# A shifted-window attention and depthwise-convolution kernel: how the first image is brought in, and where one normalization per image stands

## The chip, the cores and the metric

The kernel runs on one core of a Trainium2 chip. The metric is the device time of one execution in microseconds; the executions of a kernel are summed up by their median. A core has TensorE (PE, with weight loads PEld), VectorE (DVE), ScalarE (ACT), GpSimd (POOL) and SyncE (SP). Each engine runs its own instructions in the order in which the program has them. SP, ACT and POOL also issue DMA transfers.

## The reference

The input `x` has shape 16 x 56 x 56 x 384 in float32. Two layers follow each other, each with a residual:

```
x = x + attention(group_norm(x))     # 32 groups of 12 channels, statistics per image
x = x + depthwise(group_norm(x))     # 3x3, kernel clipped to [-1, 1] and made binary

attention(x):
    x = roll(x, (-3, -3))
    q, k, v = x @ w_qkv.T            # 12 heads of 32
    per 7x7 window: softmax(q k^T / sqrt(32) + rel_pos_table[POS] + mask) v
    out = roll(out @ w_out.T + b_out, (3, 3))
```

The statistics of the first norm need a whole image, so nothing of an image's attention starts before all of it has been read.

## The kernel before

An image is cut into eight strips (`NS`) of seven rows; strip `s` of the program is strip `s % 8` of image `s // 8`. Channels lie on the partitions, in three blocks (`NC`) of 128. A strip has eight windows, worked on in two halves, so the main loop runs over 256 half strips `u`.

`fetch(s)` reads a strip from memory into one of two landing tiles `xls` by transfers on SP's queue: six for most strips, twelve for the last strip of an image, because the shift wraps it around the image. `load(s, c)` turns it to channel-major on TensorE (`pl`), copies it to `xs` on ScalarE, and takes statistics on VectorE.

The norm of an image has two parts. `norm_gather` combines the statistics on VectorE and moves them through DRAM (`mvd`, then `gt`), so that the twelve channels of a group lie on one partition. `norm_scale` does the arithmetic of a group on GpSimd, and moves scale and shift back through DRAM (`cod`, then `coef`).

The start, in program order: clear the unused part of the landing tiles and fetch strips 0 and 1; clear the padded tiles (`clear_more`); load the relative position table row by row (`load_bias`: 49 transfers of one row, one that doubles the rows, and two for the mask, all on GpSimd's queue); load strips 0 to 7, each followed by the fetch two strips on, with the weights' twelve transfers after the last fetch; gather and norm of image 0 on SP's queue; transposes of the weights (`load_weights`: per block three TensorE transposes and one copy, eight of the twelve copies on VectorE, four on ScalarE); the depthwise taps (`load_depthwise`: one transfer for the taps and three for the output bias on ScalarE's queue, six VectorE operations, a transpose, a copy); the bias additions; then `normalize(0)` on ScalarE and the first query and key matmuls.

In the main loop, `heavy(u)` gives a list of slots of work for TensorE, and `run` issues them one by one. After the first three slots stands a transpose of the attention weights each (`pp`); after slot three stands `attend`, which multiplies by the values (`po`) and copies the output `ot` on ScalarE. Before slot 0 stands `scores(u + 1)`; before the third transpose stands `softmax(u + 1)`. "Light" work, from a plan with due times, goes behind the slot in which it falls due: a due time `w` goes out when `w - u` is at most `(i + 1) / slots`. The plan holds the fetches and loads of the next image (`plan_load`) and the convolution of the image before (`plan_conv`).

In the second half of a strip the first three slots hold the value matmuls of the next strip. Three more hold the projection of the strip before, unless the strip is the first of an image. `normalize(s + 2)`, three ScalarE operations that write `xn`, stands in the fifth slot (index `NC + 1`). Where the strip is the first of an image, the list has two empty slots in place of the projection, and the normalization comes in the last of five slots, after `attend`. This happens once per image, at `u = 16 b + 1`.

Of the kernel before, what the change touches and what calls it, by code (L numbers as in the profile page):

```python
# [9 lines left out]
F32 = mybir.dt.float32  # L10
AF = mybir.ActivationFunctionType
ALU = mybir.AluOpType
AX = mybir.AxisListType

WIN = 7
SHIFT = WIN // 2
GROUPS = 32
# [16 lines left out]
def kernel(  # L34
# [12 lines left out]
    nc = tc.nc  # L47
# [60 lines left out]

    hps = [const.tile([P, BR + 2, W + 2], F32, tag=f"hp{n}", name=f"hp{n}") for n in range(2)]

    def clear():
        for xl in xls:
            nc.gpsimd.memset(xl[:, NL - 1, :], 0.0)

    def clear_more():
        nc.gpsimd.memset(power, -0.5)
        for t in (xn, qk[:, :, ST:], vt, *es, *hps):
            nc.gpsimd.memset(t, 0.0)

    staged = []  # L120

    def fetch_weights():

        rows = [w[r * P : (r + 1) * P, :] for w in (w_qkv, w_out) for r in range(w.shape[0] // P)]
        for n in range(0, len(rows), NC):
            wl = xpool.tile([P, NC, ST], F32, tag="x", name=f"wl_{n}")
            for k in range(NC):
                nc.sync.dma_start(wl[:, k, :C], rows[n + k])
            staged.append(wl)
# [27 lines left out]

    loaded_bias = []

    def load_bias():  # L160

        rel = ypool.tile([P, NC, WIN, R], F32, tag="y", name="rel").rearrange("q c h w -> q (c h w)")[:, : T * NH]
        nc.gpsimd.memset(rel, 0.0)
        flat = rel.rearrange("q (a n) -> q a n", a=WIN)
        for q in range(T):
            qr, qc = divmod(q, WIN)
            first = (WIN - 1 - qr) * REL + (WIN - 1 - qc)
            row = rel_table[first : first + 1, :]
            src = bass.AP(
                tensor=row.tensor,  # L170
                offset=row.offset,
                ap=[[NH, 1], [REL * NH, WIN], [1, WIN * NH]],
            )
            nc.gpsimd.dma_start(flat[q : q + 1], src)
        nc.gpsimd.dma_start(flat[HT : HT + T], flat[0:T])
        mask = ypool.tile([P, NC, WIN, R], F32, tag="y", name="mask").rearrange("q c h w -> q (c h w)")[:, : 2 * T]
        mask = mask.rearrange("q (v k) -> q v k", v=2)
        nc.gpsimd.memset(mask, 0.0)
        for w in range(2):
            nc.gpsimd.dma_start(mask[w * HT : w * HT + T], wmask[0:T, :, 0:T])  # L180
        loaded_bias[:] = [rel, mask]

    def add_bias():
        rel, mask = loaded_bias
# [14 lines left out]
    def norm_gather(key, queue):  # L199

        st = stats.pop(key)
        name = "%d_%d" % key
        mv = small.tile([P, NC, 2], F32, tag="mv", name=f"mv{name}")
        for c in range(NC):
            nc.vector.bn_aggr(mv[:, c, :], st[:, c].rearrange("p s k -> p (s k)"))
        if key[0]:
            nc.vector.tensor_tensor(mv[:, :, 0], mv[:, :, 0], bo_sb, ALU.add)
        by_channel = dram.tile([C, 2], F32, tag="mvd", name=f"mvd{name}")
        queue.dma_start(by_channel.rearrange("(c p) k -> p c k", p=P), mv)
        gt = small.tile([GROUPS, GS, 2], F32, tag="gt", name=f"gt{name}")  # L210
        queue.dma_start(gt.rearrange("g n k -> g (n k)"), by_channel.rearrange("(g n) k -> g (n k)", n=GS))
        parts[key] = gt

    def norm_scale(key, queue):

        gt = parts.pop(key)
        name = "%d_%d" % key
        g = small.tile([GROUPS, 4], F32, tag="g", name=f"g{name}")
        mean, var, rstd, shift = (g[:, n : n + 1] for n in range(4))
        dev = small.tile([GROUPS, GS], F32, tag="dev", name=f"dev{name}")  # L220
        pool = nc.gpsimd

        def fold(x):

            n = GS
            while n > 1:
                half = n // 2
                pool.tensor_tensor(x[:, :half], x[:, :half], x[:, n - half : n], ALU.add)
                n -= half

        pool.tensor_copy(dev, gt[:, :, 0])
        fold(dev)
        pool.tensor_scalar(mean, dev[:, 0:1], 1.0 / GS, None, ALU.mult)
        pool.tensor_tensor(dev, gt[:, :, 0], mean.to_broadcast([GROUPS, GS]), ALU.subtract)
        pool.tensor_tensor(dev, dev, dev, ALU.mult)
        pool.tensor_tensor(dev, dev, gt[:, :, 1], ALU.add)
        fold(dev)
        pool.tensor_scalar(var, dev[:, 0:1], 1.0 / GS, EPS, ALU.mult, ALU.add)
        pool.tensor_tensor(rstd, var, power[:GROUPS], ALU.pow)
        pool.tensor_tensor(shift, mean, rstd, ALU.mult)  # L240
        pool.tensor_scalar(shift, shift, -1.0, None, ALU.mult)
        both = small.tile([GROUPS, GS, 2], F32, tag="both", name=f"both{name}")
        pool.tensor_copy(both, g[:, 2:4].unsqueeze(1).to_broadcast([GROUPS, GS, 2]))
        by_channel = dram.tile([C, 2], F32, tag="cod", name=f"cod{name}")
        queue.dma_start(by_channel.rearrange("(g n) k -> g (n k)", n=GS), both.rearrange("g n k -> g (n k)"))
        coef = small.tile([P, NC, 2], F32, tag="coef", name=f"coef{name}", bufs=4)
        queue.dma_start(coef, by_channel.rearrange("(c p) k -> p c k", p=P))
        coefs[key] = coef
# [3 lines left out]

    xs = {}

    def fetch(s):
        b, r = divmod(s, NS)
        xl = xls[s % 2]
        first = r * WIN + SHIFT
        for odd in range(2):
            t, end = 0, (WIN + 1 - odd) // 2  # L260
            while t < end:
                row = (first + odd + 2 * t) % H
                n = min(end - t, (H - row + 1) // 2)
                rows = x[b, row : row + 2 * n - 1 : 2].rearrange("t w c -> w t c")
                here = xl[odd * W : (odd + 1) * W, t : t + n, :]
                for lo, hi in ((SHIFT, SHIFT + 48), (SHIFT + 48, W), (W, R)):
                    nc.sync.dma_start(here[lo - SHIFT : hi - SHIFT], rows[lo % W : (hi - 1) % W + 1])
                t += n

    def load(s, c):  # L270
        b, r = divmod(s, NS)
        if (0, b) not in stats:
            stats[0, b] = small.tile([P, NC, NS, 6], F32, tag="st0", name=f"st0_{b}", bufs=1)
        if c == 0:
            xs[s] = xpool.tile([P, NC, ST], F32, tag="x", name=f"x_{s}")
        pt = bank(f"pl_{s}_{c}")
        for t in range(NL):

            n = min(LT, max(ST - t * LT, HT + 1))
            nc.tensor.transpose(  # L280
                pt[:, t * LT : t * LT + n], xls[s % 2][:n, t, c * P : (c + 1) * P], ident[:n, :n]
            )
        nc.scalar.copy(  # L283
            xs[s][:, c, :].rearrange("p (w r c) -> p r w c", r=WIN, c=WIN),
            pt[:, :ST].rearrange("p (r w c) -> p r w c", w=NW, c=WIN),
        )
        nc.vector.bn_stats(stats[0, b][:, c, r, :], xs[s][:, c, :])  # L287
# [286 lines left out]
    def heavy(u):  # L574

        s, half = divmod(u, UPS)
        if half == 0:
            todo = [[] for _ in range(2 * NC)]
            if s + 1 < B * NS:
                for m in range(2 * NC):  # L580
                    todo[m].append((query_key, (s + 1, m)))
            for n, m in enumerate((0, 1, 4, 5)):
                todo[m].append((by_key, (s, n)))
            if s > 0 and s % NS == 0:
                todo += [[(project, (s - 1, m))] for m in range(NC)]
        else:
            todo = [[] for _ in range(NC)]
            if s + 1 < B * NS:
                for m in range(NC):
                    todo[m].append((value, (s + 1, m)))  # L590
            if s > 0 and s % NS:
                todo += [[(project, (s - 1, m))] for m in range(NC)]
            else:
                todo += [[], []]
            if s + 2 < B * NS:
                todo[NC + 1].append((normalize, (s + 2,)))
        return todo

    def run(todo):
# [3 lines left out]

    with tc.manual_schedule():
        clear()
        fetch(0)
        fetch(1)
        clear_more()
        load_bias()
        for s in range(NS):  # L610
            for c in range(NC):
                load(s, c)
            if s + 2 < NS:
                fetch(s + 2)
            if s + 2 == NS - 1:
                fetch_weights()
        norm_gather((0, 0), nc.sync)
        norm_scale((0, 0), nc.sync)
        for n in range(NC + 1):
            load_weights(n)  # L620
        load_depthwise()
# [78 lines left out]
```

## Time and profile before

| What | Value |
|---|---|
| Median of four executions | 4734.1 us (4730.68 to 4735.7) |
| The profiled execution | 4730.68 us, span 4728.9 us |
| Busy share of the span | PE 96%, PEld 63%, DVE 84%, ACT 52%, POOL 11% |
| Mean granted TensorE clock | 0.979 |
| First transfer of a strip issued | 1.33 us |
| Statistics ready, `mvd` issued | 41.85 us |
| Group arithmetic on GpSimd | 50.29 to 56.75 us |
| First query matmul (`pq`) | 60.85 us |

In the lines of the profile, times are microseconds from the start of the span. A group names its line in the code, the engine, the operation, the output and the inputs, and how often it occurs; the bracket at the end holds the idle time of the engine before it and what ended that. "Issue" is time in which an engine waited for nothing that the profile shows. A busy TensorE is not one at full speed, since matmuls are pipelined.

### The profile page before, as it was taken

To read this page: it belongs to the slowest core of one execution; us is meant where nothing else is said; L and a number is where in the kernel's file an instruction comes from. 1 tells how busy PE (TensorE), PEld (TensorE's weight loads), DVE (VectorE), ACT (ScalarE), POOL (GpSimd) and SP (SyncE) were. 2 spreads that over 40 slices of the span, in tenths; PEclk is the share of its full clock that TensorE was granted. 3 is DMA by queue.
4 is the path that set the end of the run, shared out by engine and by line. 5 is a ranking of instruction groups with operands and counts; after the bars stand their busy time and mean duration, and the time that the engine had idled before them with its cause. 6 is when DMAs were issued, how large, how long until landed. Compare 5 with 4: busy or idle time off the path is not lost.

```text
span 4728.9 us, 146228 instructions
## 1 busy us (share of the span) xinstructions
PE 4527.0 (96%) x65895; PEld 2997.2 (63%) x65895; DVE 3951.6 (84%) x4367; ACT 2473.4 (52%) x4805; POOL 527.5 (11%) x1214
## 2 busy tenths in 40 slices
PE   6999999999999999999999999999999999999981
PEld 4666666666666666666666666666666666666651
DVE  4557888888888888888888888888888888888898
ACT  3445555555555555555555555555555555555543
POOL 3001110111101011110111101011110111101000
PEclk9999999999999999999999999999999999999995
DMA  3112222222222323223232222223223232222223
GB/s 75 48 28 60 79 63 84 68 70 83 68 66 79 80 63 84 66 71 88 60 78 83 63 70 79 79 64 84 65 72 88 60 78 83 68 65 67 63 68 95
DMA packets 168067, 337.71 MB, mean 71 GB/s; under 512 B 24290, under 2 KB 126187, under 8 KB 167442
## 3 DMA queue, kind: packets, MB, share of 16 engines
q1 hardware_dynamic: 142528, 246.48, 20.2%
q0 software_dynamic: 24464, 81.86, 4.9%
q8 instruction: 517, 8.47, 0.8%
q14 instruction: 108, 0.88, 0.1%
q10 hardware_dynamic: 450, 0.02, 0.0%
HBM read 169.69 MB, written 158.47 MB: 69 GB/s over the span
## 4 chain that ended last, share of the span: by engine, by line
PE 93%; DVE 3%; ACT 2%; issue 1%; DMA 1%; POOL 0%; SPq 0%; ACTq 0%; DVEq 0%; POOLq 0%
PE pq L307 34%; PE pv L320 17%; PE py L429 16%; PE ps L351 6%; PE pp L386 6%; PE po L407 5%; PE pk L333 4%; PE pl L280 3%; PE px L528 3%; DVE o L517 2%; DMA xl<-in_x_dram 0%; ACT e L375 0%; ACT hp L492 0%; ACT pt L392 0%; DMA mvd<-mv 0%
## 5 line engine op out<-in xcount | busy, mean ns | idle before, releaser
L307 PE MATMUL pq<-xn,wq_t 128*128 128x392 f32 x4608 | 1700.5, 504 | 26.6 <-ACT xn L296 17.6
L517 DVE SCALAR_TENSOR_TENSOR o<-hp,dw_t,o 128x784 f32<-128x784 f32 x1536 | 1572.6, 1026 | 29.9 <-ACT o L504 10.7
L307 PEld LDWEIGHTS pq<-xn,wq_t 128*128 128x128 f32 x4608 | 816.2, 190 | 488.3 <-ACT xn L296 24.8
L314 ACT COPY qk<-pq 128x392 f32<-128x392 f32 x768 | 373.7, 487 | 1149.7 <-PE pq L307 1147.9
L320 PE MATMUL pv<-xn,wq_t 128*128 128x392 f32 x2304 | 840.3, 499 | 0.0
L429 PE MATMUL py<-ot,wo_t 128*128 128x392 f32 x2304 | 814.5, 499 | 0.3 <-ACT xo L529 0.3
L377 DVE TENSOR_REDUCE total<-e 128x24 f32<-128x1176 f32 x256 | 352.6, 1377 | 371.6 <-ACT e L375 370.8
L429 PEld LDWEIGHTS py<-ot,wo_t 128*128 128x128 f32 x2304 | 417.4, 190 | 258.8 <-ACT ot L416 2.4
L320 PEld LDWEIGHTS pv<-xn,wq_t 128*128 128x128 f32 x2304 | 404.0, 188 | 224.7
L327 ACT COPY vt<-pv 128x392 f32<-128x392 f32 x384 | 190.0, 495 | 623.9 <-PE pv L320 623.9
L386 PEld LDWEIGHTS pp<-ident,e 113*128 113x128 f32 x3072 | 356.6, 140 | 174.4 <-issue 100.0
L359 DVE SCALAR_TENSOR_TENSOR t<-ps,bias 128x1176 f32<-128x1176 f32 x256 | 352.6, 1378 | 111.2 <-PE ps L351 111.2
L386 PE MATMUL pp<-ident,e 113*128 113x113 f32 x3072 | 423.0, 259 | 4.9 <-DVE e L380 3.5
L449 POOL COPY y<-y 128x63 f32<-128x63 f32 x128 | 32.4, 253 | 3143.9 <-DVE y L437 3143.9
L392 ACT COPY pt<-pp 128x392 f32<-128x392 f32 x768 | 370.0, 482 | 5.8 <-PE pp L386 5.2
L380 DVE TENSOR_TENSOR e<-e,inv 128x1176 f32<-128x1176 f32 x256 | 354.6, 1385 | 8.8
L370 DVE TENSOR_TENSOR t<-t,top 128x1176 f32<-128x1176 f32 x256 | 354.1, 1383 | 8.8
L369 DVE TENSOR_REDUCE top<-t 128x24 f32<-128x1176 f32 x256 | 352.8, 1378 | 8.8
L407 PEld LDWEIGHTS po<-pt,v 49*32 49x32 f32 x24576 | 246.2, 105 | 157.9 <-ACT pt L392 81.3
L351 PEld LDWEIGHTS ps<-qk 32*64 32x64 f32 x24576 | 281.7, 131 | 93.7 <-issue 59.6
L351 PE MATMUL ps<-qk 32*64 32x49 f32 x24576 | 315.1, 228 | 14.2 <-issue 14.1
L287 DVE BATCH_NORM_STATS2 st<-x 128x6 f32<-128x392 f32 x384 | 216.2, 563 | 124.2 <-ACT x L283 119.5
(79 smaller groups left out, 4347.7 us busy)
## 6 DMA issues: line engine op xcount, KB each, us to landing
mid<-y POOLq DMA_DIRECT2D x112, 619.5 KB, 4.0
out_dram<-xo SPq DMA_DIRECT2D x192, 336.0 KB
xb<-mid SPq DMA_DIRECT2D x96, 472.0 KB
xb<-mid SPq DMA_DIRECT2D x96, 442.5 KB
xl<-in_x_dram SPq DMA_DIRECT2D x112, 288.0 KB
xl<-in_x_dram SPq DMA_DIRECT2D x112, 216.0 KB
out_dram<-xo SPq DMA_DIRECT2D x64, 168.0 KB
xl<-in_x_dram SPq DMA_DIRECT2D x48, 144.0 KB
```

The source lines that it names most:

```text
L307: nc.tensor.matmul(pq[:, :ST].rearrange("p (w t) -> p w t", t=T), wq_t[:, c, m * P : (m + 1) * P], xn[:, c, :, :T], start=(c == 0), stop=( ...
L314: nc.scalar.copy(qk[:, m, :ST], pq[:, :ST])
L320: nc.tensor.matmul(pv[:, :ST].rearrange("p (w t) -> p w t", t=T), wq_t[:, c, 2 * C + m * P : 2 * C + (m + 1) * P], xn[:, c, :, :T], start= ...
L351: nc.tensor.matmul(pp[r * HT : (r + 1) * HT, i, k0 : k0 + T], qk[part, j, q0 : q0 + HT], qk[part, NC + j, q0 : q0 + T], start=True, stop=True,
L369: nc.vector.tensor_reduce(top, tr, AX.X, ALU.max)
L370: nc.vector.tensor_tensor(tr, tr, top.unsqueeze(2).to_broadcast([P, 2 * NH, T]), ALU.subtract)
L380: nc.vector.tensor_tensor(e, e, inv.unsqueeze(2).to_broadcast([P, 2 * NH, T]), ALU.mult)
L386: nc.tensor.transpose(pp[:, i * P : i * P + QT], es[u % 2][:QT, i * NC + j].rearrange("q w k -> q (w k)"), ident[:QT, :QT],)
L392: nc.scalar.copy(pt, pp.rearrange("k (n q) -> k n q", q=HT)[:, :, :T])
L407: nc.tensor.matmul(po[w][i * D : (i + 1) * D, (2 * j + r) * T : (2 * j + r + 1) * T], vs[u, r][keys, h * D : (h + 1) * D], pt[keys, 2 * i ...
L429: nc.tensor.matmul(py[:, :ST], wo_t[:, c, m * P : (m + 1) * P], ots[s][:, c, :], start=(c == 0), stop=(c == NC - 1),)
L517: nc.vector.scalar_tensor_tensor(acc, hp[:, dy : dy + BR, dx : dx + W], dw_t[:, c, t : t + 1], acc, ALU.mult, ALU.add)
```

## The change

The start and one slot of the main loop change; no other arithmetic does.

- Four tiles that are not in use until the attention starts (the two softmax tiles `es`, `xn` and `vt`) serve as landing tiles for strips 2 to 5 of the first image. Six fetches stand at the start. Strips 6 and 7 use `xls`. The last part of each of the four tiles is cleared on GpSimd beforehand; the tiles as a whole are cleared on VectorE (`clear_again`) after the norm of the first image, and no longer on GpSimd at the start.
- The relative table is loaded in two parts: 24 rows on GpSimd's queue at the start; the other 25 rows, the doubling transfer and the mask's two transfers on SP's queue, after the weights. That stands ahead of the norm's transfers on the same queue.
- The arithmetic of image 0's norm is on VectorE, but for the power, which stays on GpSimd. The other images' norms stay on GpSimd.
- In the first strip of each image, the second half's list gets one empty slot instead of two, and the normalization stands in that one: four slots instead of five, the normalization ahead of `attend`.

```diff
+    spare = [
+        *(e.rearrange("q h w k -> q (h w k)").rearrange("q (t c) -> q t c", c=C) for e in es),
+        *(a.rearrange("p c w t -> p (c w t)").rearrange("p (t c) -> p t c", c=C) for a in (xn, vt)),
+    ]
...
+        for t in spare:
+            nc.gpsimd.memset(t[:, NL - 1, :], 0.0)
...
-        for t in (xn, qk[:, :, ST:], vt, *es, *hps):
+        for t in (qk[:, :, ST:], *hps):
             nc.gpsimd.memset(t, 0.0)
+    def clear_again():
+        for t in spare:
+            nc.vector.memset(t, 0.0)
...
-    def load_bias():
+    def load_bias(queue, first_q, last_q):
...
-        for q in range(T):
+        for q in range(first_q, last_q):
...
-            nc.gpsimd.dma_start(flat[q : q + 1], src)
-        nc.gpsimd.dma_start(flat[HT : HT + T], flat[0:T])
+            queue.dma_start(flat[q : q + 1], src)
+        if last_q < T:
+            return
+        queue.dma_start(flat[HT : HT + T], flat[0:T])
...
-            nc.gpsimd.dma_start(mask[w * HT : w * HT + T], wmask[0:T, :, 0:T])
+            queue.dma_start(mask[w * HT : w * HT + T], wmask[0:T, :, 0:T])
...
-    def norm_scale(key, queue):
+    def norm_scale(key, queue, pool=nc.gpsimd):
...
-        pool.tensor_tensor(rstd, var, power[:GROUPS], ALU.pow)
+        nc.gpsimd.tensor_tensor(rstd, var, power[:GROUPS], ALU.pow)
...
+    def staging(s):
+
+        if NS > s >= 2 and s < 2 + len(spare):
+            return spare[s - 2]
+        return xls[s % 2]
...
-                todo += [[], []]
+                todo.append([])
             if s + 2 < B * NS:
-                todo[NC + 1].append((normalize, (s + 2,)))
+                todo[min(NC + 1, len(todo) - 1)].append((normalize, (s + 2,)))
...
         clear()
-        fetch(0)
-        fetch(1)
+        for s in range(2 + len(spare)):
+            fetch(s)
         clear_more()
-        load_bias()
+        load_bias(nc.gpsimd, 0, 24)
         for s in range(NS):
             for c in range(NC):
                 load(s, c)
-            if s + 2 < NS:
-                fetch(s + 2)
-            if s + 2 == NS - 1:
+            if s + 2 + len(spare) < NS:
+                fetch(s + 2 + len(spare))
+            if s == NS - 3 - len(spare):
                 fetch_weights()
+                load_bias(nc.sync, 24, T)
         norm_gather((0, 0), nc.sync)
-        norm_scale((0, 0), nc.sync)
+        norm_scale((0, 0), nc.sync, nc.vector)
+        clear_again()
         for n in range(NC + 1):
             load_weights(n)
```

More of the change, by code (lines that the diff above doesn't have):

```diff
@@ L158 @@
     loaded_bias = []
-    def load_bias():
-        rel = ypool.tile([P, NC, WIN, R], F32, tag="y", name="rel").rearrange("q c h w -> q (c h w)")[:, : T * NH]
-        nc.gpsimd.memset(rel, 0.0)
+    def load_bias(queue, first_q, last_q):
+        if not loaded_bias:
+            rel = ypool.tile([P, NC, WIN, R], F32, tag="y", name="rel").rearrange("q c h w -> q (c h w)")[:, : T * NH]
+            nc.gpsimd.memset(rel, 0.0)
+            loaded_bias.append(rel)
+        rel = loaded_bias[0]
         flat = rel.rearrange("q (a n) -> q a n", a=WIN)
-        for q in range(T):
+        for q in range(first_q, last_q):
             qr, qc = divmod(q, WIN)
@@ L179, in load_bias @@
         for w in range(2):
-            nc.gpsimd.dma_start(mask[w * HT : w * HT + T], wmask[0:T, :, 0:T])
-        loaded_bias[:] = [rel, mask]
+            queue.dma_start(mask[w * HT : w * HT + T], wmask[0:T, :, 0:T])
+        loaded_bias.append(mask)
     def add_bias():
@@ L220, in norm_scale @@
         dev = small.tile([GROUPS, GS], F32, tag="dev", name=f"dev{name}")
-        pool = nc.gpsimd
         def fold(x):
@@ L253 @@
     xs = {}
+    def staging(s):
+        if NS > s >= 2 and s < 2 + len(spare):
+            return spare[s - 2]
+        return xls[s % 2]
     def fetch(s):
         b, r = divmod(s, NS)
-        xl = xls[s % 2]
+        xl = staging(s)
         first = r * WIN + SHIFT
@@ L280, in load @@
             nc.tensor.transpose(
-                pt[:, t * LT : t * LT + n], xls[s % 2][:n, t, c * P : (c + 1) * P], ident[:n, :n]
+                pt[:, t * LT : t * LT + n], staging(s)[:n, t, c * P : (c + 1) * P], ident[:n, :n]
             )
```

## The prediction

> **What bounds the kernel now.** I read the page first, then the chain of work that ended last in order of time, then busy time and DMA share by stretches, then the start and one image boundary on the timeline.
>
> ```profile
> PE 4527.0 (96%) x65895; PEld 2997.2 (63%) x65895; DVE 3951.6 (84%) x4367; ACT 2473.4 (52%) x4805; POOL 527.5 (11%) x1214
> ...
> PE 93%; DVE 3%; ACT 2%; issue 1%; DMA 1%; POOL 0%; SPq 0%; ACTq 0%; DVEq 0%; POOLq 0%
> ```
>
> TensorE carries 93% of the chain. The edit touches none of its work, so it can only move the gaps: those before TensorE gets going and those at image boundaries. The chain of the start (start, length, what):
>
> ```profile
> 3.20 4.45 DMA xl<-in_x_dram
> ...
> 41.85 5.42 DMA mvd<-mv
> 47.28 2.94 DMA gt<-mvd
> ...
> 56.77 1.34 DMA cod<-both
> 58.13 1.84 DMA coef<-cod
> ...
> 60.85 1.67 PE pq L307 x2
> ```
>
> The first attention matmul (`pq`) starts at 60.85 us: strips until 37.4, statistics 41.8, gather 50.2, 6.5 us of GpSimd arithmetic, coefficients back at 60.0. By stretches (busy us per engine with counts, clock, DMA share, GB/s):
>
> ```profile
> 2.00:10.00 8.00, 2.22 (x12) 2.00 (x12) 0.64 (x2) 1.05 (x3) 7.68 (x10) 1.00 0.74 151
> 10.00:11.00 1.00, 0.18 (x2) 0.19 (x2) 0.90 (x2) 0.51 (x1) 1.00 (x2) 1.00 0.03 3
> 11.00:18.90 7.90, 4.32 (x24) 3.80 (x23) 2.88 (x6) 2.88 (x6) 7.28 (x15) 1.00 0.66 157
> 37.40:45.50 8.10, 7.39 (x42) 6.68 (x42) 5.75 (x13) 2.98 (x6) 2.68 (x5) 1.00 0.94 290
> ```
>
> A pair of strips moves for about 8 us, then the DMA engines rest 1 us. Only that rest is open to more strips in flight. Now the start's timeline (start, length, engine, line):
>
> ```profile
> 1.98 1.37 POOL L118 MEMSET xn<- 128x1536 f32 x1
> 40.15 1.38 SPq L128 DMA_DIRECT2D wl<-in_L_conv_w_out_dram  x3
> 46.81 0.58 ACTq L143 DMA_DIRECT2D dwl<-in_L_conv_w_dram  x1
> 50.01 0.35 DVE L147 TENSOR_SCALAR dwl<-dwl 9x384 f32<-9x384 f32 x1 [1.73 <-DMA dwl<-in_L_conv_w_dram]
> 53.80 5.14 DVE L189 TENSOR_TENSOR bias<-rel,mask 128x147 f32<-128x147 f32 x16 [0.22 <-POOL dev L236]
> ```
>
> While the gather is in flight, VectorE copies weights and prepares taps and bias. Last, one row of TensorE's waits after the start (total, times, longest):
>
> ```profile
> PE pq L307 <- ACT xn L296: 10.1, 8, 1.5
> ```
>
> and the timeline at the boundary of image 8:
>
> ```profile
> 2374.94 1.11 ACT L492 ACTIVATE hp<-xb,coef 128x840 f32<-128x840 f32 x1
> ...
> 2375.93 0.71 ACT L416 COPY ot<-po 128x294 f32<-128x294 f32 x2
> ...
> 2376.29 1.22 PE L351 MATMUL ps<-qk 32*64 32x49 f32 x96
> ...
> 2377.84 1.95 ACT L296 ACTIVATE xn<-x,coef 128x392 f32<-128x392 f32 x3
> 2378.64 2.24 PE L307 MATMUL pq<-xn,wq_t 128*128 128x392 f32 x6 [1.13 <-ACT xn L296]
> ```
>
> Eight of sixteen boundaries have this wait of 1.1 to 1.5 us. Six others stop 1.1 to 2.9 us inside `ps` for "issue", which hides it; the first two have neither.
>
> **What the skill says.** "VectorE: DVE Perf Modes", Zero memsets can be issued as uint32: one cycle per element whatever the type. The trace has no VectorE memset; GpSimd's, of the same shape, is 1.37 us. "DMA: Bandwidth & Descriptors", Issuing engines are not separate DMA queues: another issuing engine saves only sequencer time. The trace agrees: nothing waits for `rel` before 53.8. "TensorE: Matmul & The Clock Gate", Part 1: an idle TensorE falls to half clock. Here it is 0.50 from 51 to 66 us.
>
> **The change, part by part.**
>
> *Six strips.* SP had issued eight transfers by 4.21; the ninth, at 5.31, waited for a strip to land. So eight transfers, 1.3 strips, stay the window, and six strips in flight only remove the rests. A pair costs at best its bytes at the 205 GB/s seen at full share (1.204 MB, 5.9 us), at worst 7.6 us, since few-partition pieces load few engines. Four pairs from 2.2 land at 26 to 33; I take 30, against 37.4.
>
> *SP's queue.* Moved ahead of `mvd` are 25 `rel` rows, `rel<-rel` and two masks; 54 strip and 12 weight transfers were there already. Weights took 8 us (37.4 to 45.5): 37.5 now. They are issued at 0.49 us each, so issue keeps up. With eight in flight, rows 0 to 7 go out by then; 17 more at 0.32+0.04 us (the strip pieces' issue time and gap) give 43.6. `rel<-rel` waits for the last row (about 2.2 us; bounds 1.3, `cod`, and 4.1, the landing of software-queue rows): 45.8. Its issue and the masks: `mvd` at 47.0 (39 to 51), against 41.85. Behind `mvd` nothing but its own chain waits. The statistics, ready near 35, no longer matter. GpSimd's 25 rows fewer save 13 us of an engine nobody waits for.
>
> *Gather.* `mvd` took 5.42 because weight packets were ahead of it until 45.5. Later boundaries show 3.1 from issue end; I take 3.3: 50.3. `gt` 3.0: 53.3, against 50.2.
>
> *Norm on VectorE.* Before: 6.5 us. Now 14 operations at 0.16+0.03 (the 128x3 addition, 0.16), GpSimd's power 0.63 with two handovers of 0.1, three more operations 0.6: 4.1 us. Done at 57.4, against 56.8. By this step alone nothing is won or lost.
>
> *What now queues behind the gather.* VectorE runs in order, so everything that hid under the gather comes after it: four clears (`clear_again`), eight weight copies, six depthwise operations. TensorE's transposes of weights and taps precede `pq`, so `pq` waits for all. Clears: 1536 elements at 0.96 GHz, 1.6 us plus 0.06, an estimate from the skill; bounds 0.8 and 1.7; four: 6.6 (3.2 to 6.8), at 64.0. Copies: four of twelve banks were filled early, so eight rounds of three transposes (0.52 warm, twice that cold) pace it; ScalarE's last copy starts 4.2 to 6 us later, I take 5.2: 69.2. Only then ScalarE's queue issues `dwl`, 3.2 us from issue to use (46.81 to 50.01): 72.4. Six operations 2.75, transpose and start 0.6: `pq` at 75.8. Bias additions (5.1 us) hide under 15 us of `pq`. Against 60.85: **+15.0 us**. With both ends: best, `mvd` 39, clears 3.2, copies 4.2: +2.5; worst, `mvd` 51: +20. The half clock at `pq`'s start stays.
>
> *Extra memsets of slots* (four, 0.35 us pitch) end near 3 us, before strips 2 to 5 are issued; uncovered they would cost 1.4.
>
> *Boundary.* With four slots instead of five, planned pad (0.45) moves ahead of the exponential, load (0.60) and middle (0.71) stay behind it, and `xn` then precedes the `ot` copies. ScalarE from exponential to first `xn` chunk: 1.2+0.47+0.53+1.07+0.72 less overlaps = 3.7 us; TensorE is ready for `pq` 3.7 us after it (1236.06 to 1239.74). The wait goes. `ot` comes 1.9 us later and its banks are wanted 2 us after `pq` begins, so hidden by `pq`; uncovered, up to 1.9. Eight waits 10.1 us, plus 1.6 us of half clock after one, less 0.2 left at each: **-10** (-5 to -14). The "issue" stops stay.
>
> Sum: +15-10=**+5 us** on the profiled execution (4730.7, span 4728.9). That is the fastest of four; on the median 4734.1 the forecast is 4739.
>
> **Rivals.** *The gather slips further (slower).* Its place is SP's queue: if rows are paced by landing, eight per 4.1 us, 25 take 12.8 us rather than 9, and strips land at 33. `mvd` near 54, start +22, total +12: 4746. It decides once `mvd` is issued after 51.5. For it: the 4.1 row; against: that row is the software queue's.
>
> *The boundary turns into another wait.* The pad (1.10) must fit ScalarE's 1.37 us of idleness before the third `vt` copy; 0.27 is spare. Otherwise the exponential, and `po` behind it, slip and the gain is gone: +15, 4749.
>
> *The start hardly loses (faster).* Strips at the weights' 290 GB/s, `mvd` at 39, clears at half price: +4; boundaries -14: 4724. Against: full share moved strips at 205.
>
> *Six strips change nothing*, because the window stays eight: strips at 36, start +21, total +11; that is inside the first rival.
>
> **Numbers.** About 0.2% (9.5 us) can be told from no change. Forecast 0.50 (its own range 4730 to 4743, no change), gather slips 0.22, boundary lost 0.15, both slower, start hardly loses 0.13, nearly all of it faster. Range 4725 to 4751 leaves out about 0.15.
>
> **What would show it.** Strips landed near 30; `mvd` near 47; VectorE waiting for `gt`, then memsets of about 1.65 us and weight copies after 60; `pq` near 76; no `xn` wait at boundaries. The forecast is wrong if `pq` starts before 66, or if TensorE waits for `pt` or "issue" more than now.

## The result and the profile after

The changed kernel takes 4741.94 us (median of 41 executions, 4738.73 to 4747.39); the kernel before, measured beside it, 4735.22 us (61 executions, 4728.28 to 4744.32). The ratio is 1.0014, 95% interval 1.0010 to 1.0019: 6.6 us longer, which is clear of zero but less than the 0.2% set as the bound. The forecast was +5 us. That agreement is of a sum; parts of it were further off than the sum, as shown below.

The profiled execution took 4744.49 us with a span of 4742.7 us, 13.8 us more than the profiled one before. Single executions lie up to 16 us apart before and 9 after, so this pair is used for *where* time goes, and the medians for how much.

First the share of the chain by engine, from the page of the kernel after:

```profile
span 4742.7 us, 146261 instructions
...
PE 89%; DVE 5%; issue 3%; ACT 1%; DMA 1%; POOL 1%; DVEq 0%; ACTq 0%; POOLq 0%; SPq 0%
```

TensorE had 93% of the chain before. One stretch of "issue" in this chain, 46.1 us from 21.5 to 67.7, lies in the start; that is most of what "issue" has grown by. VectorE's two points are not the start, where the chain holds some 8 us of it: in the main loop this chain takes another way than the one before. So the shares alone don't say what the change cost. Stretches of the start after the change (busy us per engine, clock, DMA share, GB/s):

```profile
2.00:10.00 8.00, 2.18 (x12) 2.00 (x12) 0.59 (x2) 1.04 (x3) 7.70 (x17) 1.00 0.84 180
10.00:18.00 8.00, 4.52 (x25) 4.00 (x24) 3.46 (x7) 3.08 (x6) 5.57 (x11) 1.00 0.71 167
18.00:26.00 8.00, 4.50 (x25) 4.00 (x24) 4.49 (x8) 3.59 (x7) 3.25 (x7) 1.00 0.74 177
26.00:31.50 5.50, 4.37 (x26) 4.02 (x26) 3.22 (x6) 2.98 (x6) 0.00 (x0) 1.00 0.47 130
31.50:39.00 7.50, 4.32 (x30) 2.77 (x28) 2.33 (x7) 2.28 (x5) 0.00 (x0) 1.00 0.94 310
39.00:56.00 17.00, 0.00 (x0) 0.00 (x0) 0.00 (x0) 0.00 (x0) 0.00 (x0) 0.53 0.03 5
```

The rests between pairs are gone and the weights start 6 us earlier. But six strips "under way" raised the rate only from the 151 to 157 GB/s inside a pair of strips to 167 to 180, and for the last strips it was 130. From 39 to 56 us no engine computes and the DMA engines are 3% busy: the whole core waits for something that moves hardly any bytes. The timeline of the start says for what:

```profile
33.98 0.82 DVE L222 BATCH_NORM_AGGREGATE mv<-st 128x2 f32<-128x48 f32 x3
...
36.17 19.11 SPq L189 DMA_DIRECT2D rel<-_conv_rel_pos_table_dram  x25
...
56.87 0.76 SPq L192 DMA_DIRECT2D rel<-rel  x1
57.68 1.63 SPq L197 DMA_DIRECT2D mask<-in_wmask_dram  x2
59.35 0.45 SPq L226 DMA_DIRECT2D mvd<-mv  x1
63.11 0.34 SPq L228 DMA_DIRECT2D gt<-mvd  x1
65.06 0.16 DVE L247 COPY dev<-gt 32x12 f32<-32x12 f32 x1 [30.26 <-DMA gt<-mvd]
...
68.86 0.32 SPq L261 DMA_DIRECT2D cod<-both  x1
69.30 1.34 DVE L130 MEMSET e<- 128x1536 f32 x1 [0.47 <-issue]
...
74.12 1.34 DVE L130 MEMSET vt<- 128x1536 f32 x1 [0.27 <-issue]
...
79.43 0.58 ACTq L155 DMA_DIRECT2D dwl<-in_L_conv_w_dram  x1
...
81.00 0.35 DVE L159 TENSOR_SCALAR dwl<-dwl 9x384 f32<-9x384 f32 x1 [0.38 <-DMA dwl<-in_L_conv_w_dram]
...
84.27 1.02 PE L329 MATMUL pq<-xn,wq_t 128*128 128x392 f32 x1
```

SP spends 19.11 us issuing 25 table rows, 0.76 us each, while the statistics lie ready at 34.8 us. `mvd` goes out at 59.35 instead of 41.85. VectorE stands for 30.26 us before the gathered statistics, with the clears, the copies and the taps behind it; they run from 69.3 to 84. The first query matmul starts at 84.27 us instead of 60.85, **23.4 us later**.

What is won back shows in the lag of the later kernel: the start of the copy that closes each strip (`y`, GpSimd), after minus before, at the first strip of each image (images are counted from 0):

```
image   0    1    2    3    4    5    6    7    8    9   10   11   12   13   14   15
lag  22.6 22.2 21.2 20.3 17.8 19.7 20.8 18.1 16.9 15.5 14.3 13.0 14.0 12.8 11.5 13.4  us
```

The lag falls in steps, most of them at the image boundaries, by 9.2 us in all. TensorE's wait for `xn` no longer appears in the list of its waits; before, it stood at images 4, 5, 7, 8, 10, 11, 13 and 14. At seven of these the lag fell by 1.2 to 2.7 us, 11.4 together. At the eighth, image 5, another stop took its place. Boundary of image 8 on the timeline, after:

```profile
2393.99 1.22 PE L373 MATMUL ps<-qk 32*64 32x49 f32 x96
...
2394.34 1.93 ACT L318 ACTIVATE xn<-x,coef 128x392 f32<-128x392 f32 x3
...
2395.14 2.25 PE L329 MATMUL pq<-xn,wq_t 128*128 128x392 f32 x6
...
2396.16 0.69 ACT L438 COPY ot<-po 128x294 f32<-128x294 f32 x2
```

The normalization now precedes the `ot` copies, and `pq` follows `ps` without a gap. Not everything went. These are waits of TensorE after the change and, last, one from before (total, times, longest):

```profile
PE ps L373 <- issue: 15.4, 8, 3.2
...
PE py L451 <- ACT vt L349: 2.7, 1, 2.7
...
PE pq L329 <- ACT x L305: 2.2, 1, 2.2
...
PE ps L351 <- issue: 14.1, 8, 2.9
```

At images 5, 6, 12 and 15 the lag steps up. At image 5 it is the stop of 2.2 us before `pq`, followed by 3.4 us of half clock; the copy that this stop is put down to had been done for 1 us, so its cause isn't shown. At images 12 and 15 the "issue" stop in `ps` is longer than before: 3.2 us for 2.2, and 2.8 for 1.1. At image 6 that stop is as before (2.3 for 2.2), and the step isn't explained.

These stops differ between executions. Against the same trace of the kernel before, the same lag falls by 11.4 to 19.5 us in the ten kernels below that have the new boundary, and by 1.4 in the one that has the old one. The profiled execution after the change has the smallest fall of the eleven; that is in line with the medians' +6.6 lying below the +13.8 of the two traces.

### The profile page after: what moved, and what is told of

It is laid out like the page before. It is cut to its first block, busy times and chain, and to the rows that moved or that the text cites. A ratio compares the mean times of both kernels' runs of the same rounds, so it can differ in the third digit from the quotient of the medians.

```text
span 4742.7 us, 146261 instructions
## 1 busy us (share of the span) xinstructions
PE 4523.5 (95%) x65895; PEld 2995.5 (63%) x65895; DVE 3958.9 (83%) x4388; ACT 2472.0 (52%) x4805; POOL 498.9 (11%) x1169
## 4 chain that ended last, share of the span: by engine, by line
PE 89%; DVE 5%; issue 3%; ACT 1%; DMA 1%; POOL 1%; DVEq 0%; ACTq 0%; POOLq 0%; SPq 0%
PE pq L329 32%; PE py L451 16%; PE pv L342 16%; PE ps L373 6%; PE pp L408 6%; PE po L429 5%; PE pk L355 3%; DVE o L539 3%; PE px L550 3%; PE pl L302 2%; DVE top L391 0%; DVE t L392 0%; DVE t L381 0%; ACT pt L414 0%; DMA mvd<-mv 0%
## 5 line engine op out<-in xcount | busy, mean ns | idle before, releaser
L373 PE MATMUL ps<-qk 32*64 32x49 f32 x24576 | 314.3, 228 | 15.4 <-issue 15.4
L397 ACT ACTIVATE e<-t 128x1176 f32<-128x1176 f32 x256 | 309.2, 1208 | 9.8 <-DVE t L392 9.7
```

Source lines behind the costliest of these rows:

```text
L373: nc.tensor.matmul(pp[r * HT : (r + 1) * HT, i, k0 : k0 + T], qk[part, j, q0 : q0 + HT], qk[part, NC + j, q0 : q0 + T], start=True, stop=True,
```

## The experiments

All times are compared with the kernel before on the same chip. Times across experiments are compared by their ratios.

**The start alone, and the boundary alone.** Do the two halves of the change add up?

```diff
 e1_start_only (from the kernel after)
-                todo.append([])
+                todo += [[], []]
...
-                todo[min(NC + 1, len(todo) - 1)].append((normalize, (s + 2,)))
+                todo[NC + 1].append((normalize, (s + 2,)))
 e2_boundary_only (from the kernel before): the same two lines, the other way
```

> The start as changed, the boundary as before. My theory (the start costs, the boundary gives): the first query matmul at 84 us as with the whole change, and nothing won back later: in the profile 22 to 24 us longer than the kernel before, ratio 1.0047 to 1.005; the eight waits for xn of 1.1 to 1.5 us are there. Rival (the start's delay is partly made up later, since VectorE and the transfers run ahead meanwhile): ratio 1.001 to 1.003 with no boundary edit at all.

> The boundary as changed, the start as before. My theory: the first query matmul at 61 us, no wait of TensorE for xn after the start, 9 to 10 us shorter by the step-down of the lag in the trace, ratio 0.998. Rival (by the two medians, 6.7 us apart where the two profiled starts are 23 us apart, the boundary gives more than the trace shows): 16 us, ratio 0.9966. If the wait only moves: ratio 0.9995 to 1.0005.

The start alone: 4751.34 us against 4729.26, ratio 1.0044 (1.0032 to 1.0057), `pq` at 84.74. The boundary alone: 4719.58 us against 4729.26, ratio 0.9979 (0.9971 to 0.9987), and no wait for `xn` after the start. Its first `pq` came at 62.91, 2 us later than before although the start is the same: so far can the start of two single traces lie apart. In the start-alone kernel the waits are there as before the change:

```profile
PE pq L329 <- ACT xn L318: 10.8, 9, 1.5
```

By these ratios the start costs 21 us (15 to 27) and the boundary gives 10 us (6 to 14); together +11, where the whole change measured +6.6 (4.7 to 9.0). The intervals allow that the halves add up. The start's rival, 1.001 to 1.003, is out: a delay of 24 us at the first matmul is still 21 us at the end. That 3 us of it are made up stays possible. The boundary's rival, 16 us, is out of its interval.

**The table rows off SP's queue.** This undoes only the split of the rows.

```diff
-        load_bias(nc.gpsimd, 0, 24)
+        load_bias(nc.gpsimd, 0, T)
...
-                load_bias(nc.sync, 24, T)
```

> The whole change, but all 49 table rows, their doubling and the masks on GpSimd's queue. My theory (SP's 25 rows at 0.76 us each hold the gather): mvd issued at 36 instead of 59.4, landing at 41 with the weights ahead of it, gt at 44, norm done 48, clears to 54.6, the first query matmul near 63.5; ratio to the kernel before 0.998 to 0.9995. Rival (the gather waits for the rows' bytes, not for SP's sequencer, or the serial VectorE work sets the start anyway): the first query matmul stays above 75.

```profile
36.66 0.38 SPq L226 DMA_DIRECT2D mvd<-mv  x1
...
40.97 0.33 SPq L228 DMA_DIRECT2D gt<-mvd  x1
43.85 0.16 DVE L247 COPY dev<-gt 32x12 f32<-32x12 f32 x1 [7.22 <-DMA gt<-mvd]
...
62.93 0.50 PEld L329 LDWEIGHTS pq<-xn,wq_t 128*128 128x128 f32 x2
```

Each number came within 1 us of the expectation: `mvd` at 36.66, `pq` at 62.93, 21.3 us earlier than with the rows on SP. Time 4720.82 us, ratio 0.9982 (0.9975 to 0.9990). With the rows put back, the change as a whole becomes faster than the kernel before, by 0.2%. But its start gains nothing: `pq` comes where the boundary-alone kernel with the old start had it (62.91), although the statistics are ready 5 us earlier. That the order on VectorE eats these 5 us is the next question.

**The order on VectorE.** The rows stay on SP; clears, weight copies and taps stand ahead of the norm.

```diff
-        norm_scale((0, 0), nc.sync, nc.vector)
         clear_again()
         for n in range(NC + 1):
             load_weights(n)
         load_depthwise()
+        norm_scale((0, 0), nc.sync, nc.vector)
```

> The whole change, but clears, weight copies and taps stand ahead of the norm's arithmetic on VectorE; the rows stay on SP. My theory (the order on VectorE costs 11 us by itself): mvd still at 59, gt at 65, norm done at 69, coefficients at 72, the first query matmul near 73; ratio to the kernel before 0.9985 to 1.0000. Rival (the order is hidden, what comes after the norm would have waited anyway): the first query matmul stays at 84.

```profile
40.56 1.34 DVE L130 MEMSET vt<- 128x1536 f32 x1 [0.27 <-issue]
...
64.55 0.16 DVE L247 COPY dev<-gt 32x12 f32<-32x12 f32 x1 [13.31 <-DMA gt<-mvd]
...
71.66 1.94 ACT L318 ACTIVATE xn<-x,coef 128x392 f32<-128x392 f32 x3 [25.32 <-DMA coef<-cod]
72.43 0.50 PEld L329 LDWEIGHTS pq<-xn,wq_t 128*128 128x128 f32 x2 [21.51 <-ACT xn L318]
```

`pq` starts at 72.43, 11.8 us earlier than after the change, with `mvd` still at 59.20. All that used to hide under the gather hides there again, done by 51. Time 4726.28 us, ratio 0.9993 (0.9985 to 1.0001), not told apart from the kernel before. Rows and order are two separate faults: mending either alone brings `pq` forward, by 21 and by 12 us, with the other still there. Mended together, in a start further down that changes more besides, they bring 29 us rather than the sum of 33.

**What makes a row dear on SP.** Three kernels vary the form of the 25 transfers and nothing else in the start; each was timed once. In the second and third the rows hold other numbers than the table's, so only the issuing and the start are read from them.

```diff
 e8_rows_in_two: four pieces, then three, of 84 numbers each
+                for lo, hi in ((0, 4), (4, WIN)):
+                    part = bass.AP(tensor=row.tensor, offset=row.offset + lo * REL * NH,
+                        ap=[[NH, 1], [REL * NH, hi - lo], [1, WIN * NH]])
+                    queue.dma_start(flat[q : q + 1, lo:hi], part)
 e10_rows_one_run: one run of 588 numbers
+                run = bass.AP(tensor=row.tensor, offset=row.offset, ap=[[NH, 1], [1, WIN * WIN * NH]])
+                queue.dma_start(rel[q : q + 1], run)
 e11_rows_three_partitions: four pieces to each of three partitions
+                part = bass.AP(tensor=row.tensor, offset=row.offset,
+                    ap=[[NH, 3], [REL * NH, 4], [1, WIN * NH]])
+                queue.dma_start(flat[to : to + 3, 0:4], part)
```

> The whole change, but each of the 25 rows on SP's queue is sent as two transfers, of four and of three pieces of 336 bytes; same bytes, same values. It asks what makes a row cost 0.69 us of SP. If each transfer has that cost whatever it holds: 50 transfers of about 0.7, mvd near 78. If a transfer costs by its pieces: 0.4 and 0.3, mvd near 60. If seven pieces are a dear number: 0.3 each as the strips' small parts, mvd near 58 or earlier.

> The whole change, but each of the 25 rows on SP is one contiguous run of the same 2352 bytes; the values of these rows are not the table's, so the bias is left wrong. If the pieces make a row dear on SP: 0.3 us each, mvd near 48. If a transfer into a single partition is dear whatever it holds: 0.6 to 0.7 us each, mvd near 58.

> The whole change, but each of the 25 transfers on SP writes four pieces of 336 bytes to three partitions, the form of the strips' small parts, which took 0.24 to 0.32 us; the bias is left wrong. If the single partition makes a row dear: 0.3 us each, mvd near 48. If the 336-byte pieces or the table as a source do: 0.6 us or more each, mvd near 58 or later.

The groups of these transfers on SP (shortest, median, longest in ns), first after the change:

```profile
L189 SPq DMA_DIRECT2D rel<-_conv_rel_pos_table_dram x25: 692/693/884, 36.2 to 54.6; - x25
```

in two transfers a row:

```profile
L196 SPq DMA_DIRECT2D rel<-_conv_rel_pos_table_dram x50: 612/681/739, 35.8 to 70.3; - x50
```

as one run:

```profile
L191 SPq DMA_DIRECT2D rel<-_conv_rel_pos_table_dram x25: 223/250/251, 35.5 to 45.0; - x25
```

and to three partitions:

```profile
L196 SPq DMA_DIRECT2D rel<-_conv_rel_pos_table_dram x25: 241/276/281, 36.2 to 46.4; - x25
```

A transfer of three or four pieces costs about as much as one of seven, so it isn't the count of pieces. One run into a single partition costs 0.25 us, so it isn't the single partition; four pieces to each of three partitions cost 0.28 us, so it isn't pieces of 336 bytes or the table as a source. Dear, at 0.61 to 0.88 us, are several separate pieces into one partition. Why, these runs don't show, and other counts were not tried. With cheap rows `mvd` went out at 49.40 (one run) and 50.80 (three partitions), and `pq` started at 74.04 and 75.26. In the kernel with two transfers a row `mvd` went out at 74.95.

**The start in another order.** Rows on GpSimd, taps and output bias fetched at the very start, weight copies and taps under the gather, then the norm, then the clears with `xn` first.

```diff
-        load_bias(nc.gpsimd, 0, 24)
+        fetch_depthwise()          # the four transfers of load_depthwise, on ScalarE's queue
...
+        load_bias(nc.gpsimd, 0, T)
...
         norm_gather((0, 0), nc.sync)
-        norm_scale((0, 0), nc.sync, nc.vector)
-        clear_again()
         for n in range(NC + 1):
             load_weights(n)
         load_depthwise()
+        norm_scale((0, 0), nc.sync, nc.vector)
+        clear_again()              # xn, vt, then the two softmax tiles
```

> The whole change with its start put in another order: all table rows on GpSimd's queue, the transfers of taps and output bias at the very start, weight copies and taps under the gather, then the norm's arithmetic on VectorE, then the clears, xn first. My theory: gt lands at 44, norm done 48, coefficients 51.5, the first query matmul at 52 to 53, so 8 us earlier than before and 10 us from the boundary: ratio to the kernel before 0.9955 to 0.997. Rival (the clears or the weights hold it once the order is mended): the first query matmul at 58 or later, ratio 0.998.

```profile
37.69 0.38 SPq L231 DMA_DIRECT2D mvd<-mv  x1
...
42.98 0.33 SPq L233 DMA_DIRECT2D gt<-mvd  x1
...
51.24 0.32 SPq L266 DMA_DIRECT2D cod<-both  x1
...
55.44 0.50 PEld L334 LDWEIGHTS pq<-xn,wq_t 128*128 128x128 f32 x2 [8.25 <-ACT xn L323]
```

Time 4711.2 us against 4729.69, ratio 0.9962 (0.9949 to 0.9974): faster than both kernels. `pq` starts at 55.44, 5.4 us earlier than before rather than 8, since `mvd` needs 5.3 us with the weights' bytes ahead of it and the norm, behind the taps on VectorE, starts at 47.43.

**Two parts of the change within that order.** Two strips under way (`staging` gives `xls[s % 2]` and two fetches stand at the start), and the norm on GpSimd (`norm_scale((0, 0), nc.sync)`).

> As the reordered start, but strips of image 0 land in two tiles, two under way, as before. My theory (eight transfers are the window; six strips only remove the rests, worth 6 us of statistics): statistics at 41.8 instead of 35.8, the first query matmul 5 to 6 us later than in the reordered start, ratio to the kernel before 0.9965 to 0.9985. Rival (the strips are hidden behind the weights' transfer, which the gather stands behind): less than 2 us later.

> As the reordered start, but the arithmetic of image 0's norm on GpSimd. My theory: 6.5 to 7 us instead of 3.8, the first query matmul 2.5 to 3 us later than in the reordered start. Rival (GpSimd is slowed by the clears on VectorE meanwhile, or still busy with the table's rows): 5 us or more later.

With two strips `pq` starts at 61.15, 5.7 us later; time 4715.73 us, ratio 0.9971 (0.9960 to 0.9983). By the trace six strips are worth 5.7 us of start. The two intervals overlap, so the times alone don't show it; but 5.7 us is more than the 2 us by which two traces of one start lay apart.

With the norm on GpSimd its arithmetic ran from 46.12 to 51.81, 5.7 us; `pq` started at 56.03, 0.6 us later, and the time is the same: 4710.86 us, ratio 0.9962 (0.9948 to 0.9976). My 2.5 to 3 us did not come: here GpSimd began at 46.12, while in the other kernel VectorE, with the taps ahead of the norm, began at 47.43. In this order, moving the norm to VectorE gained nothing that can be measured.

**The gather on another queue.** `norm_gather((0, 0), nc.scalar)`, and the norm ahead of the taps.

> The reordered start, with the gather's two transfers on ScalarE's queue, so that they don't stand behind the weights' bytes on SP's, and the norm's arithmetic ahead of the taps on VectorE. My theory (in the reordered start the gather took 5.3 us because of the weights ahead of it): mvd 36 to 39.5, gt to 42.5, the first query matmul near 52.5 instead of 55.4; ratio to the kernel before 0.995 to 0.9965. Rival (the queues share the engines' time, so the weights delay it all the same, and ScalarE, held by the wait for mvd, copies weights later): 55 us or later.

```profile
38.05 0.39 ACTq L231 DMA_DIRECT2D mvd<-mv  x1
...
44.25 0.34 ACTq L233 DMA_DIRECT2D gt<-mvd  x1
44.63 1.24 ACT L151 COPY wq_t<-pw 128x384 f32<-128x384 f32 x3 [7.95 <-DMA mvd<-mv]
```

The rival was right: on its own queue `mvd` took 6.2 us, no less than the 5.3 behind the weights on SP's, and ScalarE waited 7.95 us with weight copies behind it. `pq` started at 58.11; the normalization before it waited last for the clear of `xn`, which stood behind the norm and the late taps on VectorE. The time, 4714.6 us, ratio 0.9959 (0.9946 to 0.9973), can't be told from the reordered start's. The slow `mvd` agrees with what the Trainium skill says in "DMA: Bandwidth & Descriptors", Issuing engines are not separate DMA queues: all transfers end on the same 16 engines. While `mvd` was under way these were 84% busy here; in the kernel after the change, at 11%, it took 3.8 us. The prediction had put beside that page that nothing waits for `rel` before 53.8. That was no trial of it, and it isn't exact: GpSimd's doubling transfer had waited 3.40 us for the last row.

## Why the prediction was right, and where it was not

*The sum.* Start +15 and boundary -10 gave +5; measured +6.6. In the traces `pq` came 23.4 us later and the lag then fell by 9.2. The start was undersized by 8.4 us, beyond the worst value I had given it (+20). Two of the five signs that I named failed with it: `mvd` near 47 (59.35) and `pq` near 76 (84.27). By the two traces, +13.8, the change is nearer to my first rival's +12 than to the forecast's +5; it is the medians that lie near the forecast. That nearness is luck: 8 us of a term were missing, and single executions scatter by as much.

*Six strips*: held. The rests went, and SP still stopped after its eighth transfer (issued at 3.87, the ninth at 5.11); the last strip's transposes began at 31.25 instead of 37.49, for a forecast of 30 for its landing.

*SP's queue*: the term of the sum that failed. I gave a row the issue time of the strips' pieces, 0.32+0.04 us; it measured 0.69+0.07. So 25 rows took 19.1 us, the last was out at 55.3 instead of 43.6, and `mvd` went out at 59.35, not 47.0 (39 to 51). The doubling and the masks took 2.5 us, for 1.2. My first rival had the right place, beyond the 51.5 at which it decides, but the wrong mechanism: it let landings pace the rows. SP waited only 0.3 us for landings; its own issuing paced them. I had no row of such a transfer on SP in the trace, and bounded the landing on both sides but not the issue. The trace did have the same row on GpSimd's queue, 15 in 8.31 us, or 0.55 each; that was a warning that I passed over.

*Gather*: 5.7 us from `mvd` to the first use of `gt`, for 6.3. *Norm on VectorE*: 3.8 us (65.06 to 68.84), for 4.1.

*What queues behind the gather*: held in kind and cost 15.4 us from the norm's end to `pq`, for 18.4. Clears ended 6.6 us after the norm, as forecast; they are recorded as 1.34 us each, 1.60 from start to start, which agrees with my 1.6 us from the one cycle per element that the Trainium skill states ("VectorE: DVE Perf Modes", Zero memsets can be issued as uint32). The copies took 4.0 us (5.2 taken). Six rounds of transposes were left, not eight, and though TensorE's granted clock was 0.50 throughout, a round took 0.68 us, not twice the warm 0.52. `dwl` landed in 1.6 us (3.2 taken, as before the change); why it took twice that before is not shown.

*The start as a sum*: 0.9 us less up to the norm's end and 3.0 us less after it, together 3.9, hid a third of the 12.4 us by which `mvd` was later than forecast; 8.4 us remain.

*Boundary*: right in mechanism, and in size as far as the times tell (-10, measured 9.7 us by itself, 6 to 14); the falls of the lag, mostly 11 to 16 us, make it rather larger. The pad fitted in front of the exponential, and that rival fell; `po` waits for `pt` a little less than before (13.2 us for 16.3). I counted 1.6 us of half clock after one of the eight waits; the trace has it after two, at images 4 and 7. The "issue" stops stayed. By the letter one sign of being wrong was met, "issue" more than before: 15.6 us for 14.6 in all, but the boundary-alone kernel had 17.3, so that 1 us says nothing.

*The fast rival* failed already at the strips' rate: 167 to 180 GB/s, not 290.

## What to carry to other kernels

A transfer that nobody waits for is not free if it stands in front of one that somebody waits for: price its issue by a transfer of the same form on the same queue. Where the trace has none, give the issue a range of its own: here the nearest price was too low by a factor of two. When arithmetic on a critical chain goes to a faster engine, list what that engine did during the waits of the chain; here 2.7 us of faster arithmetic brought 15 us of queued work behind it. Before raising the number of buffers under way, see how many transfers the queue has in flight; here SP stopped after eight with two landing tiles and with six.

## What the runs showed of the hardware

Issuing on SP a transfer of three, four or seven separate pieces into one partition took 0.61 to 0.88 us; the same bytes as one run 0.25 us, and three partitions with four pieces each 0.28 us. The mask (49 partitions) took 0.79 us and the doubling of the rows 0.76 us.

In the kernel before, TensorE stopped three times for 1.5 us before `pq`. After two of these stops, at images 4 and 7, the granted clock was 0.50 for 3.4 us, and the six matmuls that followed took 3.79 us where six took 2.24 after the stops of 1.1 us. After the third, and after the five stops of 1.1 us, it stayed full. So a short stop can cost twice its length.
